# A four-layer graph network on one core: an earlier place for layer 1's fused weights, and one head of layer 3 weighted by ScalarE

## The chip, the cores and the metric

The kernel runs on one core of one Trainium2 chip. Its time is the device time in microseconds (us) of one execution. The engines are TensorE (PE in the profile; its weight loads are PEld), VectorE (DVE), ScalarE (ACT), GpSimd (POOL) and SyncE (SP), which here only issues DMAs.

## The reference

A graph of N = 3327 nodes has features x of 512 columns and a random adjacency of about 0.24% density, thickest in the first rows. Four layers follow, each of the form `x = layernorm(x + layer(x, adj))`:

```python
# layer 0: graph attention, 8 heads of 64
Wh = einsum('nd,hdo->hno', x, W); e = leaky_relu(f1[:, :, None] + f2[:, None, :])   # f = Wh . a
out = elu(softmax(where(adj > 0, e, -9e15)) @ Wh)
# layer 1: mean over neighbours, two projections joined by a third
out = relu(concat([x @ W_self + b_self, mean_adj(x) @ W_nb + b_nb]) @ W_comb + b_comb)
# layer 2: mean over the first 64 neighbours of each row
out = leaky_relu(x @ W_line.T + b_line) + leaky_relu(mean64(x) @ W_nb.T + b_nb)
# layer 3: graph attention with a quaternion weight, 4 heads of 128
h = einsum('nf,hfo->hno', x, hamilton(W)); out = elu(softmax(where(adj > 0, e, -9e15)) @ h)
```

In layer 1 nothing stands between the two linear steps, so `x @ W_self` followed by `W_comb` can be one product with a fused weight `W_self @ W_comb[:512]`, and likewise for the neighbours.

## The kernel before, in words

Rows are worked in NB = 26 blocks of 128. The adjacency is read once, and edge lists are made from it; the aggregations then gather rows of tables in DRAM by these lists.

**The prologue** (about the first 222 us). A loop over t = 0 to 25 (L1706) advances several generators, each by one stage per iteration. `projection(t)` (L1635) loads a later block of x, transposes block t on TensorE (L789), multiplies it with layer 0's weights (L1056), and writes a block of layer 0's table `t0_d` (L1067, stored by L777). `more(3)` takes three steps of `structure` (L858), which loads a block of adjacency (L872), makes a mask of it on ScalarE (L881, L882) and builds its edge lists, mostly on VectorE (L897, L909, L919 and what follows) with small matmuls (L931 to L941, L964) between. `first_rows` (L1671, from t = 10) transposes the mask of the first rows after a scan on VectorE (L1683, L1686). `fused_weights` (L1645), begun at t = 9, makes layer 1's fused weights: its first step loads the 2 MB of `W_comb` into `wc`, the biases, and a block `raw` of `W_self`; then, for each of eight blocks, one step transposes `raw` (L789, copied by L792) and the next multiplies it with half of `wc` (`times`, L806), copies the result out (L1662) and loads the next block. A last step makes the fused bias with eight matmuls against `wc` (L1667 to L1669). The function yields 17 times. After the loop, `g0.head` and `g0.finish` take maxima over all blocks, and what is left of the fused weights is drained. `lent` places `wc` and other temporary tiles one behind the other in the memory that the gathers of layer 0 use later.

**Order.** Up to layer 1 the order of each engine's instructions is planned by the framework: the order of the text is a priority, and an instruction may be placed ahead of others where the plan finds its engine free. From L1829 on (`manual_schedule`) each engine runs the instructions in the order of the text. SyncE's queue holds nearly all plain DMAs, POOL's queue the gathers (L1018).

**Layers 0 and 3** share `Gat.group` (L1290), a generator for a group of up to four chunks of 128 edges of one row block. Stage by stage: gather the rows and compute which edge belongs to which row (L1316); the comparison that selects (L1326, VectorE); the row's own score by matmul (L1340 in layer 3); the sum of scores (L1353, L1355, VectorE) and two exponentials on ScalarE (L1356 into `w`, L1357 into the gathered rows, one per head) with a copy of the selection (L1361); the weighting of all heads of all chunks by one product on VectorE (L1364); and the matmuls that add the group to the row block's sums (L1383). One step of the main loop advances every live group by one stage, the oldest first, and then the ends of row blocks (L1411 to L1420 for the first column, L1532 to L1564 and L855 for division, elu and layernorm).

Of the kernel before, what the change touches and what calls it, by code (L numbers as in the profile page):

```python
# [17 lines left out]
AF = mybir.ActivationFunctionType  # L18
# [5 lines left out]
P = 128  # L24
# [607 lines left out]
def sparse_path(ctx, tc, flag_i, x, adj, l0_w, l0_a1, l0_a2, l1_w_self, l1_b_self, l1_w_nb, l1_b_nb,  # L632
# [13 lines left out]
    nc = tc.nc  # L646
# [21 lines left out]
    for b in range(NB):  # L668
        lists.append([])
        if b:  # L670
            n = SEGMENTS[b]
# [367 lines left out]
    class Gat:  # L1039
# [250 lines left out]
        def group(self, item, pools, accs, done, sall=None):  # L1290

            b, l, c0, g, at = item
            ring, sp, pacc, pone = pools
            H, OUT, M = self.H, self.OUT, self.M
# [18 lines left out]
            for t, k, q0, q1 in parts:  # L1313
                if q0 < q1:
                    o = t[:, q0 * P:q1 * P] if t is far else t[:, :(q1 - q0) * P]
# [5 lines left out]
            for t, k, q0, q1 in parts:  # L1321
                o, dk = ds[:, q0 * P:q1 * P], dgs[:, l.at, k:k + 1]
# [7 lines left out]
            n = 1 if self.k else 3  # L1330
            pe = pg[:, :GROUP * n * 2 * H].rearrange("p (c k h) -> p c h k", c=GROUP, k=n)
            w = pg[:, GROUP * n * 2 * H:GROUP * (2 * n + 1) * H].rearrange("p (c h) -> p c h", c=GROUP)
# [27 lines left out]
            else:  # L1360
                nc.scalar.activation(S[:, :g], have, AF.Identity)  # L1361
            yield
            Gc = G.rearrange("p c (h m) -> p (c h) m", m=M)
            nc.vector.tensor_mul(Gc[:, :, :OUT], Gc[:, :, :OUT],  # L1364
                                 w[:, :g].rearrange("p c (h o) -> p (c h) o", o=1).to_broadcast([P, g * H, OUT]))
            yield
            while self.held[self.turn] if at == 0 else b not in accs:
                yield
# [241 lines left out]
    with ExitStack() as pro:  # L1610
# [24 lines left out]
        def projection(b):  # L1635
            if b + 3 < NB:
                load(xres[b + 3], x, b + 3)
            yield
            xt = transposed(xp, ps, xres[b], g0.xsum, b)
            yield  # L1640
            pw = g0.products(ps, xt)
            yield
            g0.write(b, xp, pw)

        def fused_weights():  # L1645

            wc = lent(2 * DC * D).rearrange("p (c o) -> p c o", o=D)
            nc.sync.dma_start(wc, l1_w_comb.rearrange("(c p) o -> p c o", p=P))
            nc.sync.dma_start(bias1, row(l1_b_comb, D))
            bs = wp.tile([P, 2 * DC, 1], F32, name="bs")  # L1650
            with nc.allow_non_contiguous_dma(reason="two small biases"):
                nc.sync.dma_start(bs[:, :DC, 0], l1_b_self.rearrange("(c p) -> p c", p=P))
                nc.sync.dma_start(bs[:, DC:, 0], l1_b_nb.rearrange("(c p) -> p c", p=P))
            for s, (src, o) in enumerate(((l1_w_self, wx), (l1_w_nb, wn))):
                for i in range(DC):
                    raw = xp.tile([P, D], F32, name="raw")
                    nc.sync.dma_start(raw, src[i * P:(i + 1) * P, :])
                    yield
                    rt = transposed(xp, ps, raw)
                    yield  # L1660
                    po = times(ps, rt, wc[:, s * DC:(s + 1) * DC, :])
                    nc.scalar.copy(o[:, i, :], po)  # L1662
            yield
            pb = ps.tile([P, D], F32, name="po")
            for k in range(2 * DC):
                bb = wp.tile([P, P], F32, name="bb", bufs=2)
                nc.vector.tensor_copy(bb, bs[:, k].to_broadcast([P, P]))  # L1667
                nc.tensor.matmul(pb, bb, wc[:, k, :], start=k == 0, stop=k == 2 * DC - 1)
            nc.vector.tensor_add(bias1, pb, bias1)  # L1669

        def first_rows():  # L1671

            zeros16 = lent(3 * D, BF16)
            nc.gpsimd.memset(zeros16, 0.0)
            zero = zeros16[0:1, :]
            for r in (0, 1, ROWS - 1):
                for k in range(2):
                    nc.sync.dma_start(t1_d[r:r + 1, k * D:(k + 1) * D], zeros16[0:1, :2 * D].bitcast(F32))
                nc.sync.dma_start(t2_d[r:r + 1, :], zero)
            so_far = lent(NP, I16)  # L1680
            nc.gpsimd.memset(rows[:, free:], 0.0)
            near = so_far.bitcast(BF16)
            nc.vector.tensor_tensor_scan(so_far, m0, m0, 0.0, ALU.add, ALU.bypass)  # L1683
            for o in (row0, near0):
                if o is near0:
                    nc.vector.scalar_tensor_tensor(near, so_far, KEEP, m0, ALU.is_le, ALU.mult)  # L1686
                for c0 in range(0, NB, 8):
                    g = min(8, NB - c0)
                    yield
                    pt = banks.tile([P, 8, P], BF16, name="lp")  # L1690
                    for c in range(g):
                        src = m0 if o is row0 else near
                        nc.tensor.transpose(pt[:, c, :], src[:, (c0 + c) * P:(c0 + c + 1) * P], ident16)
                    nc.scalar.activation(o[:, c0:c0 + g, :], pt[:, :g, :], AF.Identity, saturate=False)
# [3 lines left out]
        def more(n=1):  # L1698
            nonlocal ready, whole
            for k in range(n):  # L1700
                b = next(made, None)
                whole = b is not None or ready == NB - 1
                ready = ready if b is None else b

        fused, rows01 = Stages(), Stages()
        for t in range(NB):  # L1706
            work.add(projection(t))
            work.step()
            more(3)
            if t == 9:  # L1710
                fused.add(fused_weights())
            if t == 10:
                rows01.add(first_rows())
            fused.step()
            rows01.step()
# [486 lines left out]
@with_exitstack  # L2202
def kernel(ctx: ExitStack, tc: tile.TileContext, *args):


    nc = tc.nc
    pool = ctx.enter_context(tc.tile_pool(name="flagp", bufs=1))
    flag_i = pool.tile([1, 1], I32, name="flag_i")
    sparse_path(tc, flag_i, *args)
    again = nc.values_load(flag_i[0:1, 0:1], min_val=0, max_val=1 << 20)  # L2210
    with tc.If(again > 0):
        general_path(tc, *args)
# [30 lines left out]
```

## Time and profile before

| what | value |
|---|---|
| runs | 1755.98, 1755.54 and 1752.04 us; median 1755.54 us |
| profiled execution | 1754.64 us, span of its instructions 1752.9 us |
| granted TensorE clock, mean | 0.934 of full speed |
| busy us: PE, DVE, ACT, POOL | 1510.1, 1183.2, 865.8, 748.6 |
| moved by DMA | 382.01 MB, mean 218 GB/s |

The busy time of an engine is summed over the whole span; the bound of a stage has to be read in that stage. A group of instructions is shown by line, engine and operation, the tiles out<-in, their size and number, then its busy us and the mean ns of one, and behind the second bar the idle time of the engine just before, with what ended it. A wait names the engine and line that waited, then what it waited for. A time within an execution counts from its first instruction.

### The profile page before, as it was taken

What the parts mean: (1) busy time and instruction counts of PE and PEld (TensorE: products, weight loads), DVE (VectorE), ACT (ScalarE), POOL (GpSimd) and SP (SyncE); (2) the same over time, 40 slices, a digit from 0 to 9 for tenths busy, and PEclk for the clock granted to TensorE, in tenths of its full rate; (3) what the DMA queues carried; (4) which work ended last, traced back from release to release, by engine and by line L of the source; (5) the groups of instructions that cost most, each with busy time, mean ns of one, the idle gap of its engine ahead of it and who ended that gap; (6) DMA issues with size and microseconds to landing.
All of it is one profiled execution on the core that took longest, in us unless ns stands there. A gap on an engine that the chain in (4) does not pass through costs nothing.

```text
span 1643.8 us, 24418 instructions
## 1 busy us (share of the span) xinstructions
PE 1484.8 (90%) x7307; PEld 1001.9 (61%) x7341; DVE 1183.4 (72%) x3210; ACT 865.7 (53%) x2907; POOL 754.1 (46%) x992
## 2 busy tenths in 40 slices
PE   6789968899999999989999999887999996889985
PEld 4557746666666777545555555433576764767774
DVE  7988789998567879415566677657656554889997
ACT  5779865776767778512222121212344443557786
POOL 3000047665555521055444565147765621777770
PEclk9879989999999999989999999999999997899998
DMA  8868678876665552198788999458987842888882
GB/s 254 266 235 262 199 253 282 268 221 205 201 183 159 185 146 86 52 383 310 247 301 316 322 364 341 145 173 295 307 299 230 267 150 59 247 242 254 262 252 72
DMA packets 120795, 382.01 MB, mean 232 GB/s; under 512 B 22029, under 2 KB 23669, under 8 KB 120651
## 3 DMA queue, kind: packets, MB, share of 16 engines
q0 software_dynamic: 67696, 252.97, 47.9%
q1 hardware_dynamic: 52954, 127.35, 22.9%
q8 instruction: 61, 1.00, 0.2%
q14 instruction: 84, 0.68, 0.1%
HBM read 331.89 MB, written 48.37 MB: 231 GB/s over the span
## 4 chain that ended last, share of the span: by engine, by line
PE 61%; DVE 13%; ACT 8%; DMA 7%; issue 5%; POOL 3%; SPq 0%; ACTq 0%; POOLq 0%; DVEq 0%
PE po L806 19%; PE acc L1383 11%; PE acc L1893 9%; PE po L1056 9%; PE pt L789 3%; PE acc L1271 2%; DMA gt<-t_d,idx 2%; DMA gl<-t_d,idx 1%; DVE gl L1364 1%; PE acc L1885 1%; PE acct L1491 1%; ACT h L1532 1%; DVE upc L1420 1%; DVE e L1546 1%; POOL gt L1018 1%
## 5 line engine op out<-in xcount | busy, mean ns | idle before, releaser
L1018 POOL DMA_INDIRECT gt<-t_d,idx x201 | 201.8, 1004 | 343.9 <-DVE eq L978 208.9
L1018 POOL DMA_INDIRECT gl<-t_d,idx x265 | 263.8, 996 | 149.2 <-DMA t_d<-t 45.3
L1383 PE MATMUL acc<-gt,sel 128*128 128x264 f32 (+3 forms) x804 | 209.7, 408 | 4.9 <-DVE gt L1364 3.1
L1018 POOL DMA_INDIRECT gm<-t_d,idx x140 | 140.4, 1003 | 140.0 <-PE acc L1893 95.3
L806 PE MATMUL po<-wn,xt 128*128 128x512 f32 x408 | 188.0, 602 | 3.5 <-ACT xt L792 3.5
L1383 PEld LDWEIGHTS acc<-gt,sel 128*128 128x128 f32 (+3 forms) x804 | 153.2, 199 | 42.7 <-issue 14.0
L1383 PE MATMUL acc<-gl,sel 128*128 128x260 f32 (+3 forms) x524 | 135.6, 405 | 15.9 <-issue 6.9
L1056 PE MATMUL po<-gt,xt 128*128 128x268 f32 x416 | 117.3, 426 | 13.1 <-ACT g0fall L1068 8.2
L1364 DVE TENSOR_TENSOR gt<-gt,pg 128x1536 f32<-128x1536 f32 (+3 forms) x64 | 116.6, 1822 | 13.5 <-ACT sel L1359 13.2
L806 PEld LDWEIGHTS po<-wn,xt 128*128 128x128 f32 x408 | 75.4, 191 | 81.4 <-issue 73.0
L1383 PEld LDWEIGHTS acc<-gl,sel 128*128 128x128 f32 (+3 forms) x524 | 98.7, 198 | 31.8 <-issue 7.5
L792 ACT COPY xt<-pt 128x512 f32<-128x512 f32 x80 | 46.8, 589 | 127.7 <-PE pt L789 117.1
L1893 PE MATMUL acc<-gm,selr 128*128 128x512 f32 (+3 forms) x324 | 107.7, 456 | 4.1 <-DMA gm<-t_d,idx 2.0
L909 DVE MAX8 cand<-val 128x8 f32<-128x464 uint16 (+32 forms) x184 | 107.5, 619 | 0.1
L796 ACT ACTIVATE xt<-pt 128x128 f32<-128x128 f32 (+1 forms) x208 | 55.7, 291 | 91.7 <-PE pt L789 91.4
L1056 PE MATMUL po<-w,xt 128*128 128x262 f32 x416 | 99.3, 392 | 2.8 <-DVE xt L800 1.9
L1018 POOL DMA_INDIRECT gk<-t_d,idx x65 | 65.2, 1003 | 76.7 <-PE acc L1271 53.2
L789 PE MATMUL pt<-s_ident,xres 128*128 128x128 f32 x500 | 78.3, 284 | 23.6 <-POOL rooms L1605 11.6
L1056 PEld LDWEIGHTS po<-gt,xt 128*128 128x128 f32 x416 | 78.8, 202 | 31.3 <-ACT g0fall L1068 8.6
L806 PE MATMUL po<-wx,xt 128*128 128x512 f32 x208 | 94.0, 596 | 1.5 <-ACT tb L1938 1.2
L1316 ACT ACTIVATE far<-place,sites 128x128 int16<-128x128 int16 (+3 forms) x167 | 87.3, 544 | 12.9 <-DVE ds L1326 11.8
L806 PE MATMUL po<-wl,xt 128*128 128x512 f32 x208 | 93.5, 594 | 0.6 <-ACT xt L792 0.6
(406 smaller groups left out, 3236.0 us busy)
## 6 DMA issues: line engine op xcount, KB each, us to landing
ab<-in_adj_dram SPq DMA_DIRECT2D x25, 832.0 KB
ab<-in_adj_dram SPq DMA_DIRECT2D x25, 831.5 KB
t_d<-t SPq DMA_DIRECT2D x25, 512.0 KB
gm<-t_d POOLq DMA_DIRECT2D x21, 512.0 KB
t_d<-t SPq DMA_DIRECT2D x25, 384.0 KB
t_d<-tg SPq DMA_DIRECT2D x25, 264.0 KB
gd<-t_d SPq DMA_DIRECT2D x25, 264.0 KB
t_d<-tg SPq DMA_DIRECT2D x25, 260.0 KB
```

The source lines that it names most:

```text
L789: nc.tensor.transpose(pt[:, c, :], src[:, c * P:(c + 1) * P], ident)
L792: nc.scalar.copy(xt, pt)
L796: nc.scalar.activation(xt[:, c, :n], pt[:, c, :n], AF.Identity, accum_out=xsum[:, c, b:b + 1])
L806: nc.tensor.matmul(po, xt[:, c, :], w[:, c], start=c == 0, stop=c == DC - 1)
L909: nc.vector.max(out=cand[:, s, :], in_=val[:, cuts[s]:cuts[s + 1]])
L1018: nc.gpsimd.indirect_dma_start(out=t[:m, c, :], out_offset=None, in_=table[:, :], in_offset=bass.IndirectOffsetOnAxis(ap=l.idx[:m, c0 + c: ...
L1056: nc.tensor.matmul(pw[s], xt[:, c, :], self.w[:, c, s, :], start=c == 0, stop=c == DC - 1)
L1271: nc.tensor.matmul(self.acc[h // hh][:, h % hh, :], wt[:m, h, :], G[:m, h, :], start=False, stop=False)
L1316: nc.scalar.activation(o, place[:, (c0 + q0) * P:(c0 + q1) * P], AF.Abs, bias=l.nmid[k], scale=2.0)
L1364: nc.vector.tensor_mul(Gc[:, :, :OUT], Gc[:, :, :OUT], w[:, :g].rearrange("p c (h o) -> p (c h) o", o=1).to_broadcast([P, g * H, OUT]))
L1383: nc.tensor.matmul(accs[b][s], S[:m, c, :], G[:m, c, s * hh * M:(s + 1) * hh * M], start=at + c == 0, stop=last)
L1893: nc.tensor.matmul(accs[b], chosen, parts[:, k * D:(k + 1) * D], start=at + c + k == 0, stop=k == top and at + c == n - 1)
```

## The change

The weights of layer 1 begin at t = 4 instead of t = 9. In `Gat.group`, `self.k` is 0 for layer 0 and 1 for layer 3. In layer 3 VectorE's product now leaves out the last head of the group's last chunk, and ScalarE multiplies that head, 128 columns, by the weight that it has itself written beside the row. Layer 0 keeps one product for all.

```diff
             Gc = G.rearrange("p c (h m) -> p (c h) m", m=M)
-            nc.vector.tensor_mul(Gc[:, :, :OUT], Gc[:, :, :OUT],
-                                 w[:, :g].rearrange("p c (h o) -> p (c h) o", o=1).to_broadcast([P, g * H, OUT]))
+            n = g * H - self.k
+            nc.vector.tensor_mul(Gc[:, :n, :OUT], Gc[:, :n, :OUT],
+                                 w[:, :g].rearrange("p c (h o) -> p (c h) o", o=1)[:, :n].to_broadcast([P, n, OUT]))
+            if n < g * H:
+                nc.scalar.activation(Gc[:, n, :OUT], Gc[:, n, :OUT], AF.Identity, scale=Gc[:, n, OUT:OUT + 1])
             yield
...
             more(3)
-            if t == 9:
+            if t == 4:
                 fused.add(fused_weights())
             if t == 10:
                 rows01.add(first_rows())
```

## The prediction

> **What bounds the kernel now.** I read the page first for the shares, then the window table at the two places that the change touches (the prologue, 0 to about 222 us, and layer 3, about 1467 us to the end), then the waits there, and last the chain.
>
> The window table: stretch, its length, busy us of each engine (instructions), granted TensorE clock, DMA share, GB/s.
>
> ```profile
> core 0: us, PE busy (x) PEld busy (x) DVE busy (x) ACT busy (x) POOL busy (x), PEclk, DMA share, GB/s
> 30.00:60.00 30.00, 20.27 (x119) 15.30 (x118) 27.73 (x74) 21.39 (x79) 0.00 (x0) 0.83 0.78 245
> 60.00:120.00 60.00, 50.92 (x370) 37.12 (x370) 56.87 (x233) 48.29 (x158) 0.00 (x0) 0.91 0.78 262
> 120.00:160.00 40.00, 39.61 (x256) 28.69 (x255) 32.48 (x113) 37.45 (x131) 0.00 (x0) 1.00 0.82 277
> 160.00:212.00 52.00, 50.47 (x310) 37.18 (x309) 41.86 (x145) 43.09 (x158) 0.00 (x0) 1.00 0.63 199
> 212.00:222.00 10.00, 9.52 (x44) 4.44 (x42) 9.72 (x54) 4.44 (x12) 0.65 (x1) 1.00 0.50 171
> 1640.00:1735.00 95.00, 81.44 (x531) 67.15 (x530) 88.73 (x279) 73.87 (x233) 39.35 (x41) 0.96 0.59 176
> ```
>
> The prologue changes its bound. From 30 to 120 us VectorE is 92 to 95% busy with the edge lists and TensorE has 18.8 us free; from 120 to 212 us TensorE is 98% busy and VectorE 81%. So the same TensorE work costs more after 120 us than before. In the last third of layer 3 VectorE is 93% busy and ScalarE 78%.
>
> TensorE's waits between 40 and 85 us, and ScalarE's between 1590 and 1735 us (engine, line, waited for: total us, times, longest):
>
> ```profile
> PE po L1056 <- ACT g0fall L1068: 7.9, 2, 5.0
> PE p L941 <- DVE sl L926: 3.6, 1, 3.6
> ```
> ```profile
> ACT pg L1356 <- DVE sc L1355: 10.8, 9, 1.7
> ACT pg L1356 <- PE acc L1383: 6.9, 2, 3.6
> ```
>
> The early idle of TensorE is real waiting for other engines; in layer 3 ScalarE waits for the scores from VectorE before its exponentials. The chain of 1640 to 1735 us, by line:
>
> ```profile
> by line: DVE gl L1364 16.3%; DVE upc L1420 11.2%; issue 10.7%; DMA gl<-t_d,idx 7.3%; DVE gk L1364 7.2%; DVE e L1546 6.7%; DVE h L1544 6.0%; PE acc L1383 3.5%; DVE ds L1326 3.4%; ACT h L1532 3.3%; DVE sc L1355 3.2%; DVE sc L1353 2.2%; ACT fa
> ```
>
> L1364, the product that the change shortens, holds 23.5% of it.
>
> **Layer 3, part by part.** The product has 56 instances from 1467 us on, in four sizes:
>
> ```profile
> L1364 DVE TENSOR_TENSOR gl<-gl,pg 128x1536 f32<-128x1536 f32 x24 | 41.9, 1745 | 0.5 <-ACT gl L1357 0.3 <-ACT pg L1356 0.2
> L1364 DVE TENSOR_TENSOR gl<-gl,pg 128x2048 f32<-128x2048 f32 x11 | 25.1, 2281 | 0.4 <-ACT gl L1357 0.4
> L1364 DVE TENSOR_TENSOR gl<-gl,pg 128x1024 f32<-128x1024 f32 x7 | 8.5, 1213 | 0.0
> ```
>
> 512 elements more cost 0.53 us, so 128 fewer save 0.133 us; all 56 save 7.5 us of VectorE. On the chain, 23.5% of 95 us is 22.3 us of L1364; its 25 groups there average 1.51 us, so some 15 stand on the chain. From 1590 to 1640 us the same reckoning gives one or two, from 1496 to 1590 us (5.9% of 94 us) some three. 19 times 0.133 us: **-2.5 us**.
>
> The added ScalarE instruction exists already: L1408 weights the first column's heads in the same form.
>
> ```profile
> 1466.81 1.26 ACT L1408 ACTIVATE gcol<-gcol 128x128 f32<-128x128 f32 x4
> ```
>
> One takes 0.386 us; four in 1.26 us are 0.29 us apart, which is what one costs a busy ScalarE. 56 of them: 16.2 us. Where do they fall? The instruction follows the product in the stages, so on ScalarE it stands ahead of the next group's exponentials, L1356 and L1357, whose scores come behind that product on VectorE. In one of the two groups of a row block ScalarE already waits about 1.17 us there (at 1702.37 us), and the instruction vanishes. In the other ScalarE is late (L1356 at 1706.55 us, its scores ready at 1705.44 us) and everything behind moves by 0.29 us; but ScalarE then waits again at 1709.02 to 1710.16 us, so that is absorbed. Its operands, the gathered rows and a weight that ScalarE wrote itself, are there. Behind it are queued the exponentials, the copy of the selection and the ends of the row blocks; who waits for it is the last matmul of the group, about 2 us after the product. Cost: **0**. If that cover is gone, 25 groups times 0.29 us is 7.3 us (bounds 0 and +7.3 us; the wait in ScalarE's rows makes 0 the nearer). [...] The row decides: in 1640 to 1735 us VectorE holds 93% and ScalarE 78%, 85% with 25 more instructions.
>
> **The fused weights, part by part.** A unit (eight of them) is four transposes (0.60 us), eight weight-load and matmul passes 0.43 us apart (3.44 us, one group of L806) and two copies on ScalarE (0.6 us each): 4.05 us of TensorE, 1.2 us of ScalarE. One unit takes two iterations. Its products now stand at t = 11, 13, ... 25, and then at t = 6, 8, ... 20; so three units leave t = 21 to 25 (about 165 to 206 us) for t = 6 to 10 (about 55 to 100 us), and five only change places. Behind them the bias, 16 passes of 0.43 us = 6.9 us, runs now from 212 to 221 us between the steps of the head; then it comes at t = 21.
>
> - Late side: -3 x 4.05 + 6.9 = -5.3 us of TensorE in the stretch where TensorE sets the pace. VectorE's idle 19% there leaves room.
> - Head: the maximum's transpose L1095 starts at 216.41 us behind a bias pass, its input ready about 0.8 us before, and the bias's copies on VectorE (0.22 us each) lie between the steps: -1.5 us, the first gather (221.35 us) earlier by that.
> - Early side: +12.2 us of TensorE. In 50 to 100 us its idle by tens is 5.7, 0, 2.9, 0 and 1.8 us; of these 10.4 us I count 8.7 as usable, so +3.5 us. Bounds: 0 (all of it under VectorE's 95%) and +12.2 us (none).
> - DMAs: 2048 KB of combined weights, the 256 KB bias, two small ones and eight loads of 256 KB move past five iterations of SP's queue; POOL has none in between. The first is issued at 59.18 us directly behind the load of t = 9. Behind the load of t = 4 it would be at about 38 us. There it delays adjacency halves and x by 2048 KB at 245 GB/s = 8.4 us, while VectorE runs the scan L1683 (7.09 us, from 31.05 us) and L1686 (3.6 us), which need no load: 0. Without that cover it is up to +8 us.
> - ScalarE: 3 x 1.2 us move too; it is 71 to 80% busy early: 0.
>
> Sum -5.3 - 1.5 + 3.5 = **-3.3 us**, bounds about -9 us (early side free, and the clock, 0.83 and 0.91 early, held up by fuller work) and +13 us. Layer 0 then starts that much sooner, and from 320 to 700 us TensorE is at 9 tenths nearly throughout, so it passes on.
>
> **The rivals.**
> - *No gain from the prologue.* The order before layer 1 is planned by the framework, and the text order is only a priority: the scan of L1683 is written at t = 10 and ran at 31.05 us. TensorE's work may then stay where it was, or the lists, 11 us of VectorE for each block, may set the start of layer 0's pace. For it: VectorE is busy 226 of the first 280 us. Against: raw's transposes do run two iterations apart, as written. Time: only -2.5 us, 1753.0 us.
> - *Slower: TensorE's queue stands before the combined weights.* Now they have 28 us from issue to use (59.2 to 87.0 us). After, issue at 38 us and use at about 58 us: 20 us. With two adjacency halves, x and a table block ahead or beside, 4.2 MB at 245 GB/s take 17 us. Every us beyond 20 stops the projections and the lists' matmuls queued behind. If it is 5 us late and the early idle proves unusable: -2.5 - 5.3 - 1.5 + 12.2 + 5 = +8 us, 1763.5 us. It decides as soon as the landing passes the first L806 of the new order.
> - *ScalarE becomes the bound of layer 3*: -3.3 - 2.5 + 7.3 = +1.5 us, 1757 us, within the bound below.
>
> **How the numbers follow.** 0.3% is 5.3 us, about what a measurement of this kernel can tell from no change. My case gives -5.8 us: 1754.64 us (the profiled execution, span 1752.9 us) becomes 1748.8 us; the median of the runs is 0.9 us above that execution, so 1749.7, say 1750.0 us. It has a chance of 0.5, and since it lies just past the bound, a third of it falls within; no prologue gain or a ScalarE bound have 0.25, the slow rival 0.25. Faster: 0.33 from my case and 0.1 from an early side that is free, which the other cases do not exclude: 0.43. Slower: the slow rival, mostly, 0.26. Same: 0.31. The range takes -9 with -4 (1741) as its lower end and the slow rival as its upper (1763). My case alone spans 1744 to 1755.
>
> **What would show it.** Right: the first L806 near 58 us instead of 87, the bias (L1668) gone from between the head's steps, the first gather near 218 us, TensorE's idle in 50 to 100 us halved; L1364 0.13 us shorter in layer 3 with VectorE's share of the last third falling, and 56 ScalarE instructions of 128x128 that nobody waits for. Wrong: the first gather at 221 us or later, a wait of TensorE for the combined weights before 85 us, VectorE's busy share of 60 to 120 us falling because its lists wait for TensorE, or ScalarE above 90% in layer 3 with VectorE waiting for it.

## The result and the profile after

The median of the changed kernel is 1758.97 us (17 runs, 1745.90 to 1764.28), that of the kernel before, run beside it, 1755.54 us; the ratio is 1.0016, 95% interval 0.9997 to 1.0035. The profiled execution took 1756.43 us (span 1754.7 us, clock 0.924). No difference can be told, and a gain of 5.8 us (ratio 0.9967) lies outside the interval. A repeat on another chip (e6 below) gave 0.9990 (0.9980 to 0.9999), which excludes it too. The median does fall within the stated range of 1741 to 1763 us, but in the part of it that was there for the slow rival, TensorE standing before the combined weights, and that did not happen: the range held by luck.

The window table of the changed kernel, in the columns and stretches of the table before:

```profile
30.00:60.00 30.00, 16.81 (x124) 12.98 (x124) 29.68 (x79) 18.59 (x60) 0.00 (x0) 0.76 0.90 309
60.00:120.00 60.00, 57.36 (x372) 40.85 (x372) 54.40 (x226) 50.86 (x170) 0.00 (x0) 0.92 0.67 236
120.00:160.00 40.00, 39.69 (x257) 28.23 (x258) 32.04 (x106) 37.25 (x129) 0.00 (x0) 1.00 0.80 256
160.00:212.00 52.00, 50.68 (x310) 36.88 (x309) 41.47 (x155) 40.05 (x158) 0.00 (x0) 1.00 0.56 186
212.00:222.00 10.00, 4.07 (x33) 3.15 (x32) 8.86 (x34) 7.92 (x20) 0.00 (x0) 0.72 0.92 277
1640.00:1735.00 95.00, 82.64 (x527) 66.61 (x526) 85.83 (x278) 81.10 (x260) 41.32 (x43) 0.95 0.61 181
```

From 60 to 120 us TensorE's idle time fell from 9.1 to 2.6 us, as hoped. From 30 to 60 us it rose by 3.5 us. VectorE's share from 60 to 120 us fell from 95 to 91%, which the forecast had named as a sign of being wrong. From 120 to 212 us TensorE is as full as before, although units have left this stretch. Between 212 and 222 us, where the bias ran before, it is now busy for 4.1 us instead of 9.5.

The early waits of TensorE (40 to 85 us) after the change:

```profile
PE p L941 <- DVE sl L926: 9.0, 2, 5.3
PE pt L789 <- DMA raw<-in_L_gnn_W_self_dram: 0.6, 1, 0.6
```

TensorE waits 9.0 us for the lists (3.6 before). For weights it waits 0.6 us, and that is for `raw`. The combined weights (`wc` shares a buffer that the trace calls `gt`) and the bias, from the timeline of SyncE and the instructions of L1671:

```profile
38.23 0.43 SPq L1651 DMA_DIRECT2D gt<-in_L_gnn_W_comb_dram  x1
L1671 PE MATMUL po<-gt,bb x16: 592/593/697, 176.7 to 184.6; 128*128 128x512 f32 x16
```

In layer 3, the groups of L1365 (was L1364) and of the new L1368, then ScalarE's waits and the chain by line, in the stretches of before:

```profile
L1365 DVE TENSOR_TENSOR gl<-gl,pg 128x1408 f32<-128x1408 f32 x24 | 38.7, 1611 | 0.3 <-ACT pg L1356 0.2
L1365 DVE TENSOR_TENSOR gl<-gl,pg 128x896 f32<-128x896 f32 x7 | 7.5, 1078 | 0.0
L1368 ACT ACTIVATE gl<-gl 128x128 f32<-128x128 f32 x43 | 16.6, 387 | 0.0
```
```profile
ACT pg L1356 <- PE pg L1340: 9.4, 6, 3.3
ACT pg L1356 <- DVE sc L1355: 6.3, 4, 3.5
```
```profile
by line: issue 13.7%; PE acc L1386 13.2%; DVE gl L1365 9.3%; ACT h L1535 6.5%; DVE upc L1423 5.2%; DVE e L1549 4.5%; ACT far L1316 4.3%; DVE h L1547 4.0%; ACT o L855 4.0%; ACT h L1551 3.9%; DMA gl<-t_d,idx 3.8%; ACT sel L1361 3.8%; PE pg L1
```

Each product is 0.13 us shorter. ScalarE's wait for the scores (L1355) shrank from 10.8 to 6.3 us, while its wait for the row's own score from TensorE (L1340) rose from 4.3 to 9.4 us. The product's share of the chain fell from 23.5% (both tiles) to 9.3% and what the cut line hides. In this one profile, though, layer 3 did not get shorter: from the weighting of the first column (L1411) to the last h (L1535) it took 274.5 us, 272.9 before. One row block, at 1702 us, took 9.2 us where its neighbours took 7.0 to 7.9. TensorE stood idle for 2.2 us in it, and the trace names nothing that it waited for ("issue"), so the cause is open. On the other chip (e6) layer 3 is shorter, as the table below shows.

### The profile page after: what moved, and what is told of

Same layout as the page of the kernel before. It is cut to its first block, busy times and chain, and to the rows that moved or that the text cites. A ratio compares the mean times of both kernels' runs of the same rounds, so it can differ in the third digit from the quotient of the medians.

```text
span 1642.9 us, 24468 instructions
## 1 busy us (share of the span) xinstructions
PE 1479.2 (90%) x7307; PEld 998.4 (61%) x7341; DVE 1176.9 (72%) x3210; ACT 882.3 (54%) x2964; POOL 752.6 (46%) x992
## 4 chain that ended last, share of the span: by engine, by line
PE 60%; DVE 13%; DMA 9%; ACT 8%; issue 5%; POOL 4%; SPq 0%; DVEq 0%; POOLq 0%; ACTq 0%
PE po L806 20%; PE po L1056 10%; PE acc L1386 10%; PE acc L1896 9%; DMA gl<-t_d,idx 3%; PE pt L789 3%; POOL gl L1018 2%; PE acc L1271 1%; DMA gt<-t_d,idx 1%; PE acc L1888 1%; PE acct L1494 1%; DVE cand L909 1%; DVE gt L1365 1%; DMA gk<-t_d,idx 1%; ACT h L1535 1%
## 5 line engine op out<-in xcount | busy, mean ns | idle before, releaser
L806 PE MATMUL po<-wn,xt 128*128 128x512 f32 x408 | 189.7, 606 | 3.8 <-ACT xt L792 3.8
L1386 PE MATMUL acc<-gl,sel 128*128 128x260 f32 (+3 forms) x524 | 134.4, 402 | 16.2 <-ACT gl L1368 8.4
L1365 DVE TENSOR_TENSOR gt<-gt,pg 128x1536 f32<-128x1536 f32 (+3 forms) x64 | 116.6, 1822 | 13.8 <-ACT sel L1359 13.5
L806 PEld LDWEIGHTS po<-wn,xt 128*128 128x128 f32 x408 | 76.1, 193 | 82.7 <-issue 74.0
L1056 PE MATMUL po<-gt,xt 128*128 128x268 f32 x416 | 111.8, 414 | 5.8 <-ACT m L882 2.5
L1056 PE MATMUL po<-w,xt 128*128 128x262 f32 x416 | 98.3, 390 | 3.1 <-DVE xt L800 2.2
L806 PE MATMUL po<-wx,xt 128*128 128x512 f32 x208 | 94.6, 598 | 1.6 <-ACT tb L1941 1.2
L806 PE MATMUL po<-wl,xt 128*128 128x512 f32 x208 | 93.5, 594 | 0.6 <-ACT xt L792 0.6
L1056 PEld LDWEIGHTS po<-gt,xt 128*128 128x128 f32 x416 | 78.1, 198 | 24.3 <-ACT xt L796 4.6
```

What stands on the lines that cost most here:

```text
L806: nc.tensor.matmul(po, xt[:, c, :], w[:, c], start=c == 0, stop=c == DC - 1)
L1056: nc.tensor.matmul(pw[s], xt[:, c, :], self.w[:, c, s, :], start=c == 0, stop=c == DC - 1)
L1365: nc.vector.tensor_mul(Gc[:, :n, :OUT], Gc[:, :n, :OUT], w[:, :g].rearrange("p c (h o) -> p (c h) o", o=1)[:, :n].to_broadcast([P, n, OUT]))
L1386: nc.tensor.matmul(accs[b][s], S[:m, c, :], G[:m, c, s * hh * M:(s + 1) * hh * M], start=at + c == 0, stop=last)
```

## The experiments

They ran on four chips, by the record's numbers 7 (e1 to e4), 11 (e5, e6, e8), 12 (e9 to e12) and 1 (e13); the number of the first chip is not on record. Each was timed beside the kernel before on its own chip, where that takes 1643.65 to 1644.77 us; only ratios are carried over, each with 95% interval. "Start" is the iteration at which the fused weights are begun.

**1. The two parts alone, and more than one head.** `e1`: start t = 4, layer 3 as before. `e2`: start t = 9, one head on ScalarE. `e4`: start t = 9, two heads.

```diff
-            n = g * H - self.k
+            n = g * H - 2 * self.k          # e4; 3 * self.k in e9
...
-            if n < g * H:
-                nc.scalar.activation(Gc[:, n, :OUT], Gc[:, n, :OUT], AF.Identity, scale=Gc[:, n, OUT:OUT + 1])
+            for q in range(n, g * H):
+                nc.scalar.activation(Gc[:, q, :OUT], Gc[:, q, :OUT], AF.Identity, scale=Gc[:, q, OUT:OUT + 1])
```

> The fused weights from t = 4, layer 3 as before. Theory A (the early idle of TensorE is waiting for VectorE and can't be filled, so what is moved early costs early what it saves late): last projection stored at 213 to 216 us, first gather at 221 to 225 us, total within 2 us of before, ratio 0.999 to 1.001. Theory B (the prologue's move pays and layer 3's edit eats it): layer 0 ends about 3 us earlier and the total is 3 to 6 us below before, ratio 0.9965 to 0.998. Theory C (the move alone costs): ratio above 1.002.

> One head of each group on ScalarE in layer 3, the fused weights from t = 9. Theory A (VectorE's 0.133 us per group pass on in most row blocks of the last third, minus blocks in which TensorE stands before ScalarE's head): layer 3 from the first column's weighting (1467 us) to the end 0 to 2.5 us shorter, ratio 0.9985 to 1.000. Theory B (ScalarE's head delays the last matmul of the group): layer 3 2 to 4 us longer, ratio 1.001 to 1.0025.

> Two heads of each group on ScalarE in layer 3 instead of one, the fused weights from t = 9: doubles the edit. VectorE saves 0.266 us per group, ScalarE gets 0.6 us. If one head gains and has cover, the second brings ScalarE in the last third to about 93% and the gain stops: layer 3 1 to 4 us longer than with one head. If TensorE waits for the head (Theory B) the loss doubles: ratio 1.002 to 1.005. If VectorE alone sets the pace: a further 2.5 us shorter.

> Weights from the tenth projection on, as before; in layer 3 ScalarE weights three heads of each group's last chunk. Whole layer from its column's weighting to its last h on this chip: 229.5 us with none, 226.1 and 227.9 with one, 224.6 with two. If VectorE still bounds: 222 to 223 us, ratio 0.994 to 0.9965. If ScalarE becomes the bound at three (0.29 us each, 0.87 us on a group of about 3.8 us, on top of 81 to 85%): the layer is as long as with two heads or longer, ratio over 0.9975, and the page names ScalarE as what the last chunk's matmul waits for.

> The changed kernel as it stands, beside its parts tried on one chip. If the two parts add up (0.9995 for the fused weights alone, 0.9991 for the head alone), the ratio is 0.9986 (about -2.3 us), and layer 3 from the weighting of its column to its last h is 3 to 3.5 us shorter than in a kernel with the whole product on VectorE. If the forecast's -5.8 us holds, the ratio is 0.9965. If the +3.4 us seen between the medians at first is real, that is if the two parts disturb each other, the ratio is 1.0016 or more and layer 3 is not shorter.

Measured: start alone 0.9995 (0.9980 to 1.0010), one head 0.9991 (0.9978 to 1.0003), both 0.9990, two heads 0.9965 (0.9951 to 0.9979), three heads 0.9990 (0.9977 to 1.0002). A single head cannot be told from none by the whole time, so the layer itself is read. Four heads were not measured: in a group of one chunk they would leave VectorE's product empty. The length of layer 3, from the column's weighting to the last h:

| heads on ScalarE | layer 3, us, one value for each profile | mean |
|---|---|---|
| none (e1, e3, e5, e8, e11, e12, e13) | 229.7, 229.3, 229.8, 230.2, 229.8, 231.9, 229.9 | 230.1 |
| one (e2, e6) | 226.1, 227.9 | 227.0 |
| two (e4, e10) | 224.6, 225.5 | 225.1 |
| three (e9) | 229.2 | 229.2 |

Pairs on one chip agree with the means: on chip 7 none takes 229.7 and 229.3, one 226.1, two 224.6 us; on chip 11 none takes 229.8 and 230.2, one 227.9 us; on chip 12 none takes 229.8 and 231.9, two 225.5, three 229.2 us.

ScalarE's waits for the scores from 1480 to 1620 us, and the window 1540 to 1615 us, with none, one, two and three heads, in this order:

```profile
ACT pg L1356 <- DVE sc L1355: 24.3, 18, 2.1
1540.00:1615.00 75.00, 62.55 (x432) 51.90 (x431) 70.41 (x223) 58.84 (x186) 45.33 (x47) 1.00 0.76 233
```
```profile
ACT pg L1356 <- DVE sc L1355: 14.1, 16, 1.4
1540.00:1615.00 75.00, 64.69 (x439) 53.50 (x437) 69.48 (x232) 66.52 (x214) 43.24 (x45) 0.98 0.73 226
```
```profile
ACT pg L1356 <- DVE sc L1355: 4.3, 8, 0.9
1540.00:1615.00 75.00, 64.95 (x439) 53.64 (x438) 68.62 (x229) 72.15 (x235) 42.39 (x43) 0.98 0.72 220
```
```profile
ACT pg L1356 <- DVE sc L1355: 2.9, 3, 2.1
1540.00:1615.00 75.00, 65.83 (x418) 50.80 (x418) 62.29 (x218) 73.89 (x245) 46.25 (x47) 0.95 0.76 230
```

Each of the first two heads eats some 10 us of ScalarE's wait and takes 2 to 3 us off the layer. At three the wait has nowhere to go: ScalarE is 98.5% busy, VectorE falls to 83%, and VectorE now waits for ScalarE in the ends of the row blocks. The wait of DVE h for ScalarE from 1540 to 1620 us, with two heads and with three:

```profile
DVE h L1547 <- ACT e L1545: 3.7, 8, 0.8
```
```profile
DVE h L1547 <- ACT e L1545: 9.0, 10, 1.4
```

TensorE did wait for the new instruction, though the forecast had counted on 56 instructions "that nobody waits for". Its matmuls that add full chunks from `gl` to the sums, without a head on ScalarE (e1) and with one (e2):

```profile
L1383 PE MATMUL acc<-gl,sel 128*128 128x260 f32 x476 | 117.5, 394 | 19.5 <-ACT r L1559 9.3 <-issue 7.8 <-ACT h L1532 1.0
```
```profile
L1386 PE MATMUL acc<-gl,sel 128*128 128x260 f32 x476 | 121.1, 403 | 14.9 <-ACT gl L1368 7.6 <-issue 4.3 <-ACT r L1562 1.2
```

7.6 us of idle time now end with L1368, but the sum before this group is less, 14.9 us against 19.5: a wait that replaced a longer one.

**2. What the fused weights cost in all.** `e3` leaves out the making of layer 1's fused weights and bias and loads unfused blocks in their place; start t = 9.

```diff
-                    rt = transposed(xp, ps, raw)
...
-                    po = times(ps, rt, wc[:, s * DC:(s + 1) * DC, :])
-                    nc.scalar.copy(o[:, i, :], po)
```

> Leaves out the making of the fused weights: the eight blocks are loaded straight into their place, there is no combined weight, no product and no bias product; t = 9, layer 3 as before. It prices that work: about 39 us of TensorE and 10 us of ScalarE. If TensorE's work sets the prologue after 120 us (my prediction's step), the first gather comes 15 to 25 us earlier, at 197 to 207 us. If the edge lists on VectorE set it (rival), less than 8 us earlier. What of it reaches the end tells how far an earlier start of layer 0 passes on: the prediction's step says nearly all of it; the rival, that the lists set layer 0's start, less than a third.

Measured: 0.9869 (0.9842 to 0.9895), -21.5 us, and the first gather at 204.2 us instead of 217.7 to 222.3 us. So the lists on VectorE do not set the start of layer 0 here; the making of the weights does. That it does so through TensorE's queue fits TensorE's 98% busy from 120 to 212 us, but 10 us of ScalarE and the loads left with it, and these were not parted. Of some 39 us of TensorE's work (8 x 4.05 + 6.9) about half was free where it stood.

**3. The place of the bias.** `e5`: start t = 4, the bias held back until the head has been issued. `e12`: the same hold with start t = 9. `e13`: start t = 4, the bias made twice, early (unused) and beside the head. Layer 3 as before in all.

```diff
+            while not headed:
+                yield
             pb = ps.tile([P, D], F32, name="po")
...
         g0.head(xp, ps)
         g0.finish(xp, ps)
+        headed.append(1)
```

> Weights made from the fifth projection on, but the bias (16 copies and 16 matmuls) held back until the head has been issued; layer 3 with the whole product on VectorE. If the head is set by VectorE's and ScalarE's own steps (theory now), the bias fills TensorE's gaps beside the head, the projections end some 5 us earlier than with the bias among them, the first gather is 4 to 7 us earlier than with the early bias, and the ratio is 0.9955 to 0.998. If the bias costs the head 1.5 us as the forecast took it, the first gather gains no more than 5 minus 1.5 us. If nothing in the last microseconds of the prologue reaches the first gather, the ratio is that of the early bias, 0.9995.

> Control of the 0.9948: the bias held back until the head has been issued, but the weights made from the tenth projection on, as before; layer 3 as before. If the gain came from the earlier units, which only pay while the bias stays beside the head (theory now), nothing is gained here, because the bias ran beside the head already: ratio 0.998 to 1.001, projections end at 209 to 213 us. If holding the bias back is worth 8 us by itself, whatever the start, the ratio is 0.995 again and the first gather comes at about 213 us.

> Weights from the fifth projection on, layer 3 as before; the bias is made twice: once early, as in the changed kernel, its result unused, and once more beside the head, where the result is taken. The output is the reference's. It parts the two terms of what the early bias costs: 6.9 us of TensorE's queue ahead of the last projections, and a head that was 10.4 us from the last projection product's end to the first gather with the bias early and 7.9 us with it held back. If the bias beside the head keeps VectorE's block scans out from between the head's steps, the projections end at 211 to 213 us as with the early bias, the head takes 7.5 to 8.7 us, the first gather comes at 219 to 221 us and the ratio is 0.997 to 0.999. If the head's length has another reason (the row block that VectorE has reached by then), the head takes 9.5 to 10.5 us, the first gather comes at 221.5 to 223.5 us and the ratio is 0.9995 to 1.002.

Measured: e5 0.9948 (0.9928 to 0.9968), e12 1.0010 (0.9996 to 1.0024), e13 0.9996 (0.9980 to 1.0012). The earlier start gains about 10 us against e12 if, and only if, the bias stays beside the head. A bias in front of the last projections takes it back: from e5 to e13 the ratio rises by 0.0048, 8 us. The stations of the prologue, in us:

| start, bias | last projection product ends | first gather | first product of layer 0 |
|---|---|---|---|
| t = 9, beside the head (e2, e4, e12, e9) | 213.3, 209.0, 211.4, 213.6 | 222.0, 217.7, 220.4, 222.3 | 231.0, 226.5, 229.1, 231.3 |
| t = 4, early (e1, e6, e13) | 211.9, 212.4, 213.1 | 222.3, 222.3, 222.9 | 230.9, 230.8, 232.1 |
| t = 4, beside the head (e5, e10) | 205.0, 205.9 | 212.8, 213.4 | 223.5, 223.2 |

One kernel's own place in these rows moves by some 4 us from one profile to the next (e2, e4, e12 and e9 have the same prologue or nearly so), so the means of the rows are read: the projections end 6.4 us sooner by the start, and 7.0 us later by the bias. The first gather comes at 220.6, 222.5 and 213.1 us, and at the end of layer 0 (its last block's `up`, L1532 or L1535) the rows stand at 676.0, 676.9 and 666.1 us: the gain of the third row is passed on.

The products of the projections (L1056; 16 make a block) that TensorE had started by 120 us, and the passes of the units (L806; 8 make a unit), in the first chip's profiles of before and after:

```profile
L806 PE MATMUL po<-gt,xt x16: 592/592/1202, 87.0 to 116.8; 128*128 128x512 f32 x16
L1056 PE MATMUL po<-gt,xt x200: 389/389/816, 12.3 to 119.8; 128*128 128x268 f32 x100
```
```profile
L806 PE MATMUL po<-gt,xt x32: 592/592/1062, 59.9 to 113.2; 128*128 128x512 f32 x32
L1056 PE MATMUL po<-gt,xt x193: 389/389/812, 12.4 to 119.9; 128*128 128x268 f32 x193
```

At 120 us two units more are done and 7 of 16 products of a projection fewer. This lead stays two units at 150 and at 180 us. On the other chips it is two units at 120 us as well; products by then are 199 to 211 from t = 9 and 196 to 199 from t = 4.

**4. Other places.** `e8`: start t = 14, bias as written. `e11`: start t = 4, and the last unit held back with the bias. `e10`: e5 with two heads on ScalarE. Only the held place is shown:

```diff
-            if t == 9:
+            if t == 14:                     # e8
...
                     raw = xp.tile([P, D], F32, name="raw")
+                    while s * DC + i == 2 * DC - 1 and not headed:   # e11
+                        yield
```

> Weights made from the fifteenth projection on, layer 3 with the whole product on VectorE: the same work put the other way. The forecast's reason (idle TensorE time early in the prologue that the earlier start uses) makes it later: the early side keeps its idle time, the late side holds more, +3 to +6 us, ratio 1.002 to 1.0035. If the place of this work does not matter, because what is taken from one side of the prologue is given back on the other, the ratio is within 0.002 of 1 and the table of the eighth block is stored as early as before or earlier, while the last one is stored at the same time within 3 us.

> Weights from the fifth projection on; not only the bias but also the last of the eight units (16 transposes' and products' 4 us of TensorE) held back until the head has been issued; layer 3 as before. If TensorE's queue before the head is what sets the first gather, it comes another 3 to 4 us earlier than with the bias alone held back (about 209 us), and the ratio is 0.9925 to 0.995 unless the weights then hold up the first row blocks. If the gaps beside the head are full with the bias (8.4 of 16 us between 214 and 230 us were busy there), the unit delays layer 0's first selection products by as much as it saves: ratio 0.995 to 0.997. If lists on VectorE set the pace by then, nothing changes: 0.9948.

> The two best parts together: weights from the fifth projection on with the bias held back, and two heads on ScalarE in layer 3. If they add up, as they lie in stages far apart: 0.9948 - 0.0035 = 0.9913, about 1630 us. If the second start of the bias or the shift of the stages costs layer 3 its gain: 0.9948.

Measured: e8 1.0000 (0.9988 to 1.0012), e11 0.9992 (0.9978 to 1.0006), e10 0.9921 (0.9894 to 0.9948), 1629.94 us beside 1643.85 us. e10 is 13.9 us faster than the kernel before and, by the ratios (0.9921 and 0.9990), some 11 us faster than the changed one. 0.9948 times 0.9965 is 0.9913, within e10's interval, so the two gains add up.

e11 and e8 show the other edge. TensorE's timeline, first of e5, then of e11: what is held back, and the first selection of layer 0 (L1336) behind it.

```profile
213.73 1.10 PE L1670 MATMUL po<-gt,bb 128*128 128x512 f32 x2
216.53 0.24 PE L1336 MATMUL pg<-g0own,ds 128*128 128x48 bf16 x1 [0.21 <-DVE eq L978]
```
```profile
209.86 6.44 PE L806 MATMUL po<-gt,xt 128*128 128x512 f32 x8 [0.68 <-ACT xt L792]
216.14 7.22 PE L1670 MATMUL po<-gt,bb 128*128 128x512 f32 x16
224.31 0.24 PE L1336 MATMUL pg<-g0own,ds 128*128 128x48 bf16 x1 [0.18 <-DVE ds L1326]
```

In e11 the projections end at 202.6 us and the first gather comes at 212.3 us, as early as in e5. But unit and bias then stand in TensorE's queue ahead of layer 0: its first selection comes 7.8 us later, and the first product on VectorE at 229.7 instead of 223.5 us. What VectorE lacks meanwhile, in the window 214 to 230 us of e5 and then of e11 (its third busy figure, 15.79 and 9.44 us):

```profile
214.00:230.00 16.00, 8.35 (x71) 5.95 (x71) 15.79 (x65) 13.53 (x39) 12.11 (x13) 0.62 0.90 309
```
```profile
214.00:230.00 16.00, 12.26 (x51) 5.68 (x49) 9.44 (x35) 7.33 (x21) 12.04 (x14) 0.82 0.75 215
```

In e8 two units and the bias run there (TensorE 15.03 of 16 us, VectorE 6.94), and the first product comes at 235.4 us. The gap beside the head holds the bias, whose 16 passes fit between the steps, and no more.

## Why the prediction was right or wrong

The forecast was -5.8 us; what was measured is, by the ratios, +2.8 us (-0.5 to +6.1) on the first chip and -1.6 us (-3.3 to -0.2) on chip 11. Layer 3 went as forecast on the other chips. The prologue's -3.3 us was the sum that failed: the first gather, forecast near 218 us, came at 224.17 us.

**Layer 3, -2.5 us: right, but not seen on the first chip.** The product shortened by 0.13 us, VectorE's share from 1640 to 1735 us fell from 93 to 90%, ScalarE's rose to 85% as said, and the layer is 3.1 us shorter on the other chips (230.1 to 227.0 us). On the first chip, with one profile of each kernel, it is 1.6 us longer. The cost of the ScalarE instruction was 0, because the wait named in the forecast took it in: it went from 24.3 (e1) to 14.1 us (e2). One sentence was wrong: somebody does wait for it, TensorE, but in place of a longer wait. Taken as a sum of engine time, the forecast's 16.2 us more on ScalarE for its 7.5 us less on VectorE are a loss of 8.7 us; that sum did not decide up to two heads, with which the layer is 5.0 us shorter than with none (230.1 to 225.1 us). At three, with ScalarE at 98.5%, the gain over none is almost gone; the rival "ScalarE becomes the bound" has its place there.

**Late side, forecast -5.3 us: mis-sized.** The first failed term is the three units. A start five iterations earlier at one unit for two iterations is 2.5 units, which the forecast took as three; the counts show two, at 120, 150 and 180 us. That makes -8.1 + 6.9 = -1.2 us. The +6.9 us of the bias was right in size (7.0 us between the rows of the table), and the forecast had it in its sum; what it lacked was the other choice, to leave the bias where it was. The change moves not eight units but a generator whose last step had been lying, for nothing, in gaps that only exist behind the projections.

**Head, forecast -1.5 us: wrong in sign.** From the end of the last projection product to the first gather it took 8.7 us before and 10.5 us after on the first chip; on the others 8.7 to 9.0 us against 9.8 to 10.4 us. Without the bias VectorE's scans for the lists stand between the head's steps. The timeline of VectorE in the changed kernel:

```profile
215.83 0.36 DVE L1088 TENSOR_REDUCE mx<-g0fall 128x8 f32<-128x208 f32 x1
216.10 0.82 DVE L909 MAX8 cand<-val 128x8 f32<-128x646 uint16 x1
216.84 0.15 DVE L1089 TENSOR_SCALAR mx<-mx 128x8 f32<-128x8 f32 x1
217.00 1.02 DVE L909 MAX8 cand<-val 128x8 f32<-128x832 uint16 x1
217.93 0.26 DVE L1097 TENSOR_REDUCE mc<-ptm 24x1 f32<-24x128 f32 x1
218.12 1.20 DVE L909 MAX8 cand<-val 128x8 f32<-128x1018 uint16 x1
219.25 0.21 DVE L1099 TENSOR_SCALAR dgm<-s_ident,mc 24x24 f32<-24x24 f32 x1
```

Three scans, 3.0 us, in front of three short steps. Some 0.3 us of the growth is TensorE's clock: without the bias the granted clock was 0.50 from 217 to 222 us (1.00 before), and the head's two steps on TensorE, L1095 and L1101, took 0.39 and 0.62 us instead of 0.27 and 0.40 us. That the bias had kept them out was my next theory, and e13 speaks against it: with a second bias beside the head, scans still stood between the steps and the head took 9.8 us. The likely reason, which part of a row block's list VectorE has reached by then, was not tested, so the cause of the rest stays open.

**Early side, forecast +3.5 us: right in kind, less in size.** 7 of 16 products fewer at 120 us are 7/16 of a projection's 4.5 us (3.88 us of products, 0.60 us of transposes), +2.0 us for 8.1 us of work brought forward, so about as large a part of it was free as said. The sign given for it, TensorE's idle time from 50 to 100 us halved, did not come: it fell from 10.4 to 8.4 us. On the way it looks worse: the table of the eighth block was stored at 90.5 us instead of 79.7, and the lists' matmuls waited 9.0 us, but all but 2 us came back before 120 us.

With the measured terms the sum is -1.2 + 2.0 + 1.8 = +2.6 us; the first gather came 2.8 us later (224.17 instead of 221.35 us). The head's 1.8 us is itself read from these two profiles, and places move by 4 us between profiles, so that the sum comes so close is in part chance. In the first chip's profiles this was regained in layer 0, whose last product came at 703.0 us instead of 704.5; both profiles have long waits of ScalarE from 230 to 270 us for something that the trace does not name (14.2 us before, 12.8 and 6.7 us after), so nothing is read from it. The start alone, e1, ended 0.8 us sooner, within its interval of 2.5 us, so whether such a delay reaches the end is not to be told from it.

**DMAs, 0: right.** Issue at 38.2 us and first use at 59.9 us, as said. The slower rival, TensorE waiting before the combined weights, did not occur. The rival "no gain from the prologue" came closest in its outcome, but not for its reasons: the work did move, and e3 shows that the lists alone don't set the pace.

## What to carry to other kernels

When a generator is started earlier, all its steps move, and the last one may have been standing in the only place where it cost nothing. Ask of each step, and not of the sum, which gap it lies in now, and hold that step where it was: here the bias alone turned 0.9948 into 0.9995. An engine's waits say how much it can take over: ScalarE's 24 us of waiting paid for two heads at about 10 us each and not for a third.

## What was not expected of the hardware

- The same program takes 6.3% less on the other chips: 1643.65 to 1644.77 instead of 1755.54 us. Layer 3 takes 272.9 us on the first and 229.3 to 231.9 us on the others, and the granted clock of the profiled execution was 0.934 on the first; on the others the kernel before ran at 0.952 to 0.965. Another part is waiting that only the first chip's traces hold. On the chain of the kernel before, by start and length, with nothing named that ended it:

```profile
241.91 14.14 another core or an unknown queue
1468.24 8.58 another core or an unknown queue
1477.83 15.17 another core or an unknown queue
```

That is 37.9 us, beside a difference of 111 us; the changed kernel has 60.1 us of it on its chain, and no trace of the other chips has any. What it is stays open. With waits of this size, single profiles of the first chip say little about a few microseconds of the whole time.

- In e11 work behind a thinly filled stretch of TensorE was dearer. The eight passes of a unit behind the head's waits took 6.44 us; eight in a filled stretch of e8 (from 205.21 us) took 3.60 us. This work, held back into a gap, was not to be priced by its row from a busy stretch. The windows of e11 (the granted clock is the third figure from the end):

```profile
202.00:206.00 4.00, 1.89 (x23) 1.34 (x21) 4.00 (x12) 3.76 (x14) 0.00 (x0) 0.90 0.90 270
206.00:209.80 3.80, 1.66 (x6) 1.21 (x6) 3.56 (x19) 1.55 (x4) 0.00 (x0) 0.50 0.94 332
209.80:213.00 3.20, 3.14 (x4) 1.52 (x5) 3.20 (x18) 1.09 (x3) 0.74 (x1) 0.50 0.30 123
216.20:220.00 3.80, 3.80 (x10) 1.49 (x9) 2.59 (x13) 0.89 (x2) 2.89 (x4) 1.00 0.74 193
```

TensorE was busy for less than half of the time from 202 to 209.8 us (47 and 44% in the two windows), the granted clock fell to 0.50, and the unit, begun at 209.86 us, ran at 0.50 at least until 213 us; from 216.2 to 220 us, with TensorE busy throughout, the clock was 1.00 again. The unit took 1.79 times as long as the one of e8. The longest gap of TensorE that the trace shows in the thin stretch is 1.8 us. How thin a stretch has to be, and for how long, was not tested.
